# Four two-bank PSUM tiles, and the turn of P inside the next unit's scores, in the Transformer stages of a four-layer kernel

## The chip, the core and the metric

The kernel runs on one core of a Trainium2 chip. The time is the device time of one launch in microseconds (us); a comparison uses the median of several runs. Five engines work side by side, each through its own instructions in order: TensorE (PE in the profile, its weight loads PEld), VectorE (DVE), ScalarE (ACT), GpSimd (POOL) and SyncE (SP, here the queue that issues most transfers). Matrix products are written to PSUM, which has eight banks of 128 partitions by 512 float32 values; DVE and ACT read them from there.

## The reference

Four layers of the form `x = x + s * silu(f)` run over 2048 tokens of 128 features (four rows of 512 tokens). In each, `s` comes from an attention-like function of the normalised `x` and `f` from a feed-forward-like one. In two of the layers the latter is a small local-attention Transformer of its own, and these are all that the change touches:

```python
for i in range(DEPTH):                       # third layer: 6, 16 heads, window 32; fourth: 2, 8 heads, window 64
    h = shift_tokens(x)
    q, k, v = split(h @ Wqkv[i], 3)          # heads of 64
    q, k = l2norm(q) * qs, l2norm(k) * ks    # then rotated by position
    # each window of queries sees its own window of keys and the one before
    sim  = einsum('bhwie,bhwje->bhwij', q, look(k)) * 8.0
    attn = softmax(where(mask, -max, sim))
    out  = einsum('bhwij,bhwje->bhwie', attn, look(v))
    x = x + out @ Wo[i]
    h = layernorm(shift_tokens(x)) * g + b
    a, gate = split(h @ W1[i] + b1, 2)
    x = x + (a * gelu(gate)) @ W2[i] + b2
```

Everything is float32.

## The kernel before

The layers run one after another. The Transformers are built by the class `_Transformer`, called from `transformer` (L707). Features lie on partitions, so a row of the batch is a 128x512 tile.

Work is cut into slots. A slot is one layer, one row of the batch and one group of eight heads: 6 x 4 x 2 = 48 slots in the first Transformer, 2 x 4 x 1 = 8 in the second. Three Python generators walk through the slots, each some slots behind the one before it: `queries_keys` projects q and k, sums their squares over each head by a matmul with a matrix of ones (`unit_length`), rotates them, and sends them through 16 transfers to the tiles `qk`; `attention` computes the attention of the slot before; `feed_forward` does the feed-forward of a row some slots back. In the first Transformer one slot of a pair carries the norm of the feed-forward and the other its two matmuls W1 and W2.

`merge` (L947) sets the order in which the instructions are issued. Each generator yields after some work the TensorE time that it has just put down (0.86 for a 128x512 matmul, for instance), and the one that is least advanced goes next. A scheduler then places the instructions: it keeps near this order, but lets an instruction pass another whose data or tile it does not expect to be ready, and gives each tile of a pool the buffer that it expects to be free. The semaphores follow from that. The order on each engine is fixed when the program runs.

Inside `attention` a slot has two units, `j` = 0 and 1 (four units in the second Transformer). A unit goes through these steps:

- `scores` (L1361): a mask by two bfloat16 matmuls (L1366), then 64 small matmuls (64x32 weights, 64 columns) on top of it (L1377), all into one two-bank tile; then DVE takes the maximum of each row (L1387) and subtracts it (L1391), ACT takes the exponential (L1396), DVE sums (L1398) and inverts. The result is `P`.
- `turn` (L1403): eight transposes of P (recorded at L126, names `core,l_P`) into another two-bank tile, and ACT's copy of it to `PT` (L1412).
- `weigh` (L1414): 64 small matmuls of PT with the values into a tile, which DVE normalises into `On` (L1441).
- `turn_back` (L1452): transposes of On (`core,l_On`) and ACT's copy to `OT` (L1461); after the second unit four matmuls with Wo, and DVE adds them to the row of `xn` (L1501).

At step i of its loop `attention` issues `values` (first unit only; its tile is copied to `l_vo` by ACT at L1344) and the scores of unit i, then the turn of unit i-1, the turning back of unit i-2, and the weighing of unit i-1.

Nearly all matmuls pass through the helper `mm` and are recorded at L122, so they are told apart by names: `hb,l_wqk` is a projection of q or k, `sqp,l_k` the sums of squares, `l_wv,hb` the values, `l_OT,l_wo` the output projection, `ffu,l_w` the feed-forward's W2. On DVE, L1289 and L1291 multiply a projection by the two rotation tables (`l_rot`, `rotp`) and so read its tile out; L1316 scales `l_rot` by the length. L1287 on ACT squares the projection.

In PSUM a pool `ps` holds three tiles of two banks (`S2`) and a pool `pm` two tiles of one bank (`M`): eight banks. `M` serves the output projection and W2, and in the second Transformer also the weighing and the turning back.

## Time and profile before

| | us |
|---|---|
| median of 3 runs | 4267.34 (4264.73 to 4271.99) |
| the profiled execution, its own time | 4258.36 |
| its span, first to last instruction | 4256.7 |
| TensorE busy | 3632.9 (85%) |
| VectorE busy | 2521.8 (59%) |
| ScalarE busy | 1832.3 (43%) |
| GpSimd busy | 1200.4 (28%) |
| first Transformer, about | from 1605 to 3680 |
| second Transformer, about | from 3770 to 4230 |

A line of the profile gives the source line, engine, operation, `out<-in` by the program's names, and the shape. PE's rows count a float32 matmul as two passes, so that 64 matmuls are 128 rows; a transpose is one row. Behind a row of the timeline stands in brackets the idle time of its engine before it and the instruction that ended it; "issue" is idle time with nothing in the profile that was waited for. In a list of waits the columns are the total in us, how many times, and the longest.

### The profile page before, as it was taken

How to read it: one execution, taken by the hardware profiler on the slowest of the kernel's cores; microseconds unless marked ns; L12 is line 12 of the kernel's file. 1: busy time of each engine (PE TensorE's matmuls, PEld its weight loads, DVE VectorE, ACT ScalarE, POOL GpSimd, SP SyncE). 2: the span in 40 equal slices, each digit the busy share in tenths (PEclk: the TensorE clock that was granted, in tenths of full speed). 3: DMA queues.
4: the chain of work that ended last, by engine and by line, in shares of the span. 5: the costliest groups of instructions: out<-in, count | busy, mean ns of one | idle time of the engine just before them, and what ended most of it. 6: DMA issues, size and time to landing. Idle time of an engine off the chain costs nothing.

```text
span 4256.7 us, 105246 instructions
## 1 busy us (share of the span) xinstructions
PE 3632.9 (85%) x46765; PEld 1894.8 (45%) x46891; DVE 2521.8 (59%) x3429; ACT 1832.3 (43%) x2495; POOL 1200.4 (28%) x994
## 2 busy tenths in 40 slices
PE   7887999898999986888888888888888888768888
PEld 4554555344444433444444444444444444334444
DVE  6665555205433516677677777777667676447775
ACT  3344666331333343444444444444444444424554
POOL 1011444100111224333333433343333333033221
PEclk7678999996989988999999999999999999879999
DMA  1000000000000004334233424333333332222221
GB/s 35 7 24 26 1 1 1 28 10 7 1 3 2 1 15 113 85 81 106 70 89 98 95 67 120 70 86 94 86 73 92 87 85 69 75 85 68 58 63 43
DMA packets 123574, 236.11 MB, mean 55 GB/s; under 512 B 29625, under 2 KB 44129, under 8 KB 117729
## 3 DMA queue, kind: packets, MB, share of 16 engines
q1 hardware_dynamic: 114064, 209.58, 20.3%
q10 hardware_dynamic: 8624, 19.29, 1.4%
q8 instruction: 369, 6.05, 0.6%
q0 software_dynamic: 432, 0.51, 0.1%
q14 instruction: 85, 0.69, 0.1%
HBM read 50.08 MB, written 5.54 MB: 13 GB/s over the span
## 4 chain that ended last, share of the span: by engine, by line
PE 53%; DVE 16%; ACT 16%; issue 8%; POOL 3%; DMA 3%; SPq 1%; DVEq 0%; POOLq 0%; ACTq 0%
PE S L122 29%; PE M L122 8%; PE S L126 4%; PE S L1377 3%; PE o L1092 3%; DVE l_rot L1316 3%; DVE rotp L1291 3%; ACT l_P L581 3%; DVE l_rot L1289 2%; ACT l_PT L1412 2%; PE o L614 2%; ACT rn L1312 2%; POOL l_rot L1292 2%; ACT sqp L1287 1%; ACT l_P L1396 1%
## 5 line engine op out<-in xcount | busy, mean ns | idle before, releaser
L1292 POOL TENSOR_TENSOR l_rot<-l_rot,rotp 128x1024 f32<-128x1024 f32 x224 | 533.3, 2381 | 459.1 <-DVE rotp L1291 421.6
L1288 POOL TENSOR_TENSOR sqp<-sqp 128x512 f32<-128x512 f32 x224 | 315.6, 1410 | 1010.2 <-ACT sqp L1287 1009.6
L122 PE MATMUL S<-hb,l_wqk 128*128 128x512 f32 x896 | 501.4, 659 | 108.4 <-ACT l_vo L1344 32.3
L1287 ACT ACTIVATE sqp<-S 128x1024 f32<-128x1024 f32 x224 | 229.3, 1024 | 411.0 <-PE S L122 408.6
L1316 DVE SCALAR_TENSOR_TENSOR l_rot<-rn,l_rot 128x1024 f32<-128x1024 f32 x224 | 366.2, 1672 | 64.8 <-ACT rn L1313 62.3
L1289 DVE TENSOR_TENSOR l_rot<-S,l_tab 128x1024 f32<-128x1024 f32 x224 | 272.9, 1218 | 163.7 <-ACT sqp L1287 161.8
L126 PE MATMUL S<-core,l_P 128*128 128x128 f32 x1856 | 269.5, 288 | 57.3 <-DVE rotp L1291 13.5
L122 PE MATMUL S<-l_KT,l_QT 32*128 32x256 f32 (+7 forms) x1536 | 261.9, 505 | 34.8 <-ACT l_P L1114 14.2
L126 PEld LDWEIGHTS S<-core,l_P 128*128 128x128 f32 x1856 | 211.3, 146 | 177.2 <-issue 67.4
L1291 DVE TENSOR_TENSOR rotp<-S,l_tab 128x1024 f32<-128x1024 f32 x224 | 271.6, 1213 | 22.0 <-POOL l_rot L1292 21.8
L122 PE MATMUL S<-sqp,l_k 128*128 128x512 f32 x448 | 241.7, 633 | 33.3 <-POOL sqp L1288 24.9
L1114 ACT ACTIVATE l_P<-S 128x1024 f32<-128x1024 f32 x160 | 156.7, 1022 | 254.6 <-PE S L122 254.5
L1377 PE MATMUL S<-l_qk 64*32 64x64 f32 (+1 forms) x13312 | 222.1, 236 | 43.3 <-issue 34.3
L122 PEld LDWEIGHTS S<-hb,l_wqk 128*128 128x128 f32 x896 | 150.1, 199 | 244.0 <-issue 102.2
L122 PE MATMUL S<-l_wv,hb 128*64 128x256 f32 (+1 forms) x1600 | 237.1, 403 | 7.8 <-ACT rn L1312 2.4
L1377 PEld LDWEIGHTS S<-l_qk 64*32 64x32 f32 (+1 forms) x13312 | 174.1, 110 | 154.5 <-issue 151.0
L1412 ACT COPY l_PT<-S 128x1024 f32<-128x1024 f32 x128 | 129.5, 1012 | 250.1 <-PE S L126 250.0
L1067 DVE TENSOR_REDUCE l_mx<-S 128x2 f32<-128x768 f32 (+1 forms) x192 | 154.9, 863 | 134.1 <-PE S L1006 134.1
L1398 DVE TENSOR_REDUCE rs<-l_P 128x16 f32<-128x1024 f32 (+1 forms) x128 | 155.8, 1217 | 124.2 <-ACT l_P L1396 124.1
L122 PE MATMUL M<-l_OT,l_wo 128*128 128x512 f32 (+1 forms) x512 | 222.7, 546 | 4.1 <-ACT l_OT L1461 2.2
L1118 POOL TENSOR_SCALAR_AFFINE_SELECT l_P<-l_P 128x256 f32<-128x256 f32 x256 | 99.4, 406 | 409.9 <-ACT l_P L1114 405.1
L1387 DVE TENSOR_REDUCE mx<-S 128x16 f32<-128x1024 f32 (+1 forms) x128 | 155.7, 1217 | 98.7 <-PE S L1377 98.5
(359 smaller groups left out, 6619.9 us busy)
## 6 DMA issues: line engine op xcount, KB each, us to landing
l_qk<-l_rot SPq DMA_DIRECT2D x896, 128.0 KB
l_ve<-l_vo SPq DMA_DIRECT2D x112, 256.0 KB
l_ve<-l_vo SPq DMA_DIRECT2D x96, 224.0 KB
l_tab<-in_k_rot_l ACTq DMA_DIRECT2D x16, 1024.0 KB
l_wqk<-in_l2Wqkv SPq DMA_DIRECT2D x12, 512.0 KB
l_wv<-in_l2Wqkv SPq DMA_DIRECT2D x12, 256.0 KB
l_wo<-in_l2Wo SPq DMA_DIRECT2D x12, 256.0 KB
l_ve<-l_vo SPq DMA_DIRECT2D x24, 128.0 KB
```

The source lines that it names most:

```text
L122: self.nc.tensor.matmul(out, lhsT, rhs, start=start, stop=stop)
L126: self.nc.tensor.transpose(out, in_, self.ident[:n, :n])
L1114: nc.scalar.activation(P[u], s[u], AF.Exp, scale=scale)
L1287: nc.scalar.activation(sq, p, AF.Square)
L1288: nc.gpsimd.tensor_tensor(sq[:, 0, :], sq[:, 0, :], sq[:, 1, :], ALU.add)
L1289: nc.vector.tensor_tensor(t[:, g], p, tab[:, 0], ALU.mult)
L1291: nc.vector.tensor_tensor(m, p, tab[:, 1], ALU.mult)
L1292: nc.gpsimd.tensor_tensor(t[:, g], t[:, g], m[:, ::-1, :], ALU.add)
L1316: nc.vector.scalar_tensor_tensor(t[:, g], rn[:, g, :].unsqueeze(1).to_broadcast([128, 2, S]), 1e12, t[:, g], ALU.min, ALU.mult)
L1377: net.nc.tensor.matmul(sv[W * bl : W * bl + W, e, t, g, :].rearrange("p (s k) -> p s k", s=2), qk[0][r, g, j, W * c : W * c + W], kw, star ...
L1398: nc.vector.tensor_reduce(rs, P.rearrange("p t g e k -> p (t g e) k"), axis=AX.X, op=ALU.add)
L1412: self.nc.scalar.copy(u["PT"], t)
```

## The change

The pool of single banks goes, and the two-bank pool has four tiles instead of three. `M` takes a two-bank tile and uses its first bank. `turn` is now called inside `scores`: after half of the small matmuls of unit i (32 of 64 in the first Transformer), the eight transposes of unit i-1 and ACT's copy are issued, and then the other half. Only after the last unit, when there are no more scores, is it called on its own. `turn` itself now yields the 0.9 that `attention` yielded for it.

```diff
-            pools = [pool("ps", 3, space=PSUM), pool("pm", 2, space=PSUM), pool("c"), pool("tab", 3), pool("w")]
+            pools = [pool("ps", 4, space=PSUM), pool("c"), pool("tab", 3), pool("w")]
...
     def M(self):
-        return self.PM.tile([128, 512], F32, name="M", tag="M")
+        return self.S2()[:, 0, :]
...
-    def scores(self, qk, tp, j):
+    def scores(self, qk, tp, j, last):
...
         for t in range(T):
+            if last and t == T // 2:
+                yield from self.turn(last)
             for g in range(2):
...
         self.nc.scalar.copy(u["PT"], t)
+        yield 0.9
...
-                u["P"], u["r"] = yield from self.scores(qk, tp, j)
-            if last:
-                self.turn(last)
-                yield 0.9
+                u["P"], u["r"] = yield from self.scores(qk, tp, j, last)
+            elif last:
+                yield from self.turn(last)
```

The instructions of the changed program are the same in kind and number; which stands before which, and what each waits for, is not.

## The prediction

> **What bounds the kernel now.** I read the page first (busy shares, slices), then the stretches of the two Transformers, then TensorE's waits in the steady part of the first, then one slot's timeline. Last I laid the instruction order of the changed program beside the old one, engine by engine, with the instruction that each wait hangs on; the order holds no times, so all durations are from the trace.

> ```profile
> span 4256.7 us, 105246 instructions
> PE 3632.9 (85%) x46765; PEld 1894.8 (45%) x46891; DVE 2521.8 (59%) x3429; ACT 1832.3 (43%) x2495; POOL 1200.4 (28%) x994
> ...
> PE   7887999898999986888888888888888888768888
> ```

> TensorE is the busiest engine in all 40 slices but a few, never full. By stretch:

> ```profile
> core 0: us, PE busy (x) PEld busy (x) DVE busy (x) ACT busy (x) POOL busy (x), PEclk, DMA share, GB/s
> 1700.00:3640.00 1940.00, 1671.06 (x28271) 855.64 (x28362) 1367.93 (x1469) 886.41 (x1003) 697.26 (x407) 0.98 0.36 86
> 3770.00:4230.00 460.00, 380.66 (x3008) 215.88 (x3038) 320.75 (x384) 225.32 (x279) 128.42 (x82) 0.93 0.28 70
> ```

> The first row is the steady part of the six-layer Transformer (46 slots of 42.2 us, one slot being one row of the batch for half of the heads), the second the two-layer one. The clock is already 0.98, so nothing is to be had from it. The change removes no arithmetic: it can only move TensorE's idle time, 269 us in the first stretch and 79 in the second. Where those 269 come from:

> ```profile
> PE S L122 <- issue: 59.6, 36, 4.5
> PE S L126 <- ACT l_PT L1412: 45.1, 44, 1.1
> PE S L122 <- ACT l_vo L1344: 35.2, 45, 1.1
> PE S L1377 <- issue: 30.5, 38, 4.1
> PE S L122 <- DVE rotp L1291: 27.7, 37, 1.6
> PE S L126 <- DVE rotp L1291: 17.9, 29, 4.9
> PE S L122 <- POOL sqp L1288: 12.1, 23, 1.2
> PE S L126 <- DVE l_P L1391: 11.1, 22, 0.5
> ```

> (total us, times, longest.) Once a slot or once in two, the same wait: PSUM tiles not yet read out. Here is one slot; a float32 matmul is two rows, a transpose one:

> ```profile
> 2398.75 1.98 PE L122 MATMUL S<-hb,l_wqk 128*128 128x512 f32 x4 [0.90 <-ACT l_vo L1344]
> 2400.66 0.30 PE L1377 MATMUL S<-l_qk 64*32 64x64 f32 x2
> 2400.89 1.09 PE L126 MATMUL S<-core,l_P 128*128 128x128 f32 x8
> 2403.09 0.98 PE L126 MATMUL S<-core,l_On 128*128 128x128 f32 x7 [1.10 <-ACT l_PT L1412]
> 2404.00 1.47 PE L1377 MATMUL S<-l_qk 64*32 64x64 f32 x126
> 2405.51 1.22 DVE L1387 TENSOR_REDUCE mx<-S 128x16 f32<-128x1024 f32 x1 [1.26 <-PE S L1377]
> 2406.76 1.29 DVE L1391 TENSOR_TENSOR l_P<-S,mx 128x512 f32<-128x512 f32 x2
> 2408.09 1.06 ACT L1396 ACTIVATE l_P<-l_P 128x1024 f32<-128x1024 f32 x1 [1.25 <-DVE l_P L1391]
> 2410.79 1.02 PE L1377 MATMUL S<-l_qk 64*32 64x64 f32 x78
> ```

> See two things. The turn of O stands 1.10 us behind the copy of P's turn, for want of a third two-bank tile; and from the end of a unit's scores (2405.47) to its P being ready (2409.15) there are 3.7 us of DVE and ACT.

> **The change, part by part.** Slots alternate: in "hidden" slots the feed-forward's W1 and W2 run, in "norm" slots its norm. 23 of each.

> Pool. Five tiles (three of two banks, two of one) become four of two. It adds no bank. While scores, two projections and P's turn are held, O's turn is still the fifth. So by the order:
> - Projection after the mask (35.2 us, 45 times): it now waits for the copy of the first value tile, not the second; the second is waited for later, behind a 0.86 us matmul. Gain 33.
> - O's turn (45.1 us, 44 times): in hidden slots a projection (0.86) now stands between P's turn and O's; of 1.03 about 0.2 stays: gain 18. In norm slots the two are still adjacent and wait the same: 0.
> - Projection after the sums (the rotp row; about 23 of its 37, 1.0 each): it now hangs on the addition into xn, earlier on DVE; the values behind it hang on the normalised O, 0.4 later. Gain 0.6 x 23 = 14.
> - P's turn behind rotp (17.9 us): DVE no longer does the norm's operations before that rotp in norm slots. I take 10.
> - O's turn behind the second unit's subtraction (11.1, 22 times): it now waits for P's copy, issued half a unit earlier. Gain 11.
> Sum of gains 86.

> What comes late instead:
> - In hidden slots the third W1 pair reaches TensorE earlier and meets the first GELU product, which DVE makes after two l_rot of 1.67 each: 0.5 x 23 = 11. ACT then copies the values after the last GELU and a table load of 1.28 instead of before; the l_ve transfers on SP's queue issue later with it, some 4 us, and their readers stand over 10 us further on. POOL's additions keep their order; SP's 16 l_qk transfers a slot still follow l_rot, which is no later than before. I cost the queues at nothing; if that cover went, a late l_qk would hold the scores at about 1 us a slot.
> - W2's sum and Wo's hold a two-bank tile each, so the next slot's sums and projection wait for DVE's additions; by my count DVE is done 0.9 us before. Nothing. The output projection and the weighing hang on rotp in a few places: 0.35 per two slots, 8.

> Turning P amid the scores. TensorE runs in order, so behind the transposes the other 32 scores, a sum, O's turn and the projections are queued. After the first unit's scores the old order has a mean 6.7 us of work before its P is turned (64 weighings, two projections, mask, 64 scores, a sum, part of Wo). The new order has, in hidden slots, 31 weighings (0.75), mask (0.54), a projection (1.06) and 32 scores (0.75): 3.1 against 3.7 + 0.1, a wait of 0.6: 14 us over 23. In norm slots 48 weighings and a second projection bring it to 4.6: none. In the first three slots there are 32 scores alone: 3.0 each, 9 us. The second unit's P has 20 us of cover.

> Insertions. Full-array instructions are now put amid the small ones: P's eight, and a sum beside them. By the count over both orders there are 60 more such places in the first Transformer and 19 in the second. The row for one: 16 rows of scores at 2409.46, a projection at 2409.73, scores again at 2410.79, 1.33 us for 0.16 of scores and 0.86 to 0.97 of projection (the spacings of neighbouring 128x512 pairs, 2412.68 to 2413.65 to 2414.51), so 0.2 to 0.3. [...] I take the row.

> "issue" waits. 90 us fall inside runs of small matmuls, where no semaphore is waited for, and they recur every 256 instructions. [...] I take 15 less, near the smaller of the two rows, whose place the turn now takes.

> Second Transformer, 8 slots of 55 us: cover of the third unit falls from 4.2 to 2.4 us, where it waits 1.4 already: 1.8 x 8 = 14 more; the weighing's wait for P's copy shrinks by 0.9 and a projection's (1.1) goes: 16 less; insertions 5. Net +3.

> Sum: first Transformer -86 + 11 + 8 + 14 + 9 + 15 = -29; issue -15; second +3: -41. The profiled execution took 4258.4 (span 4256.7 and 1.7 around it): 4217. The median run is 9.0 above it: 4226.

> **Rivals.**
> 1. Slower: the softmax decides. If the first unit's maximum starts late on DVE (behind rotp or a normalisation), P's turn waits in every slot with everything queued behind it. For: 3.6 us of cover are given away. Against: the maximum starts 0.04 us after the scores in nearly every old slot, and what DVE is given ahead of it is ready earlier. It decides from 0.9 us a slot above my count (41/46). At 2 us: +92 - 41 = +51, 4318.
> [...]
> 3. A larger gain: issue waits and P's wait overlap (issue -50, P's 14 gone), and the small waits that I left standing go too (-15): -41 - 35 - 14 - 15 = -105, 4162.

> **How the numbers follow.** 0.2% (8 us) is about what a measurement of this kernel can tell from no change. Forecast 0.45, taking 4190 to 4258; larger gain 0.20; no change 0.08; slower 0.27. Faster 0.65, same 0.08, slower 0.27. The forecast's own range is 4190 to 4258; for 8 in 10 it must reach near rivals 1 and 3: 4150 to 4315.

> **What would show it.** After: no l_vo row at 35 us under TensorE's waits; the l_PT row at about half of 45 us; a new row of P's turn waiting for ACT's exponential, near 14 to 23 us; issue rows below 90. TensorE's busy time should stay within 25 us of 3633. The prediction is wrong if that exponential's row passes 60 us, if issue grows, or if DVE's rotp holds the projections that now share the one pool.

## The result, and the profile after

The changed kernel takes 4204.42 us in the median (4197.12 to 4208.22, 4 runs) against 4266.03 for the kernel before (4 runs as well, one more than in the table above); the ratio is 0.9854, interval 0.9834 to 0.9874. The forecast was 4226, within 4150 to 4315: the sign and the range hold, with a gain of 62 us where 41 were forecast. What follows shows that the agreement hides an incomplete account: one half of the change gains about 100 us, and the other half, as it stands here, loses about 45 of them again.

The page of the changed kernel:

```profile
span 4203.6 us, 105187 instructions
PE 3651.2 (87%) x46764; PEld 1923.0 (46%) x46891; DVE 2504.6 (60%) x3429; ACT 1842.0 (44%) x2495; POOL 1175.8 (28%) x994
```

TensorE is busy for 18 us more, in a span 53 us shorter. To compare like with like, take each Transformer from its first to its last matmul of scores, the same work in both kernels. First the kernel before, then the changed one (first Transformer, second Transformer; columns as in the prediction):

```profile
1639.60:3647.10 2007.50, 1716.64 (x29394) 881.51 (x29487) 1409.35 (x1510) 906.40 (x1023) 721.05 (x420) 0.98 0.36 86
3815.60:4204.00 388.40, 332.91 (x2832) 193.72 (x2860) 281.86 (x340) 200.56 (x247) 104.18 (x68) 0.95 0.27 63
```

```profile
1640.40:3586.70 1946.30, 1736.13 (x29372) 906.49 (x29470) 1397.06 (x1511) 914.34 (x1023) 690.64 (x419) 0.96 0.37 89
3754.10:4155.30 401.20, 341.27 (x2836) 198.89 (x2866) 278.13 (x341) 202.50 (x247) 107.73 (x68) 0.94 0.26 62
```

The first Transformer is 61 us shorter, the second 13 longer. Note the column behind the busy times: the granted clock is 0.96 where it was 0.98. TensorE's waits in the first stretch, some of the kernel before (over this stretch, a little longer than that of the prediction), then those of the changed one:

```profile
PE S L122 <- issue: 60.6, 37, 4.5
PE S L122 <- ACT l_vo L1344: 36.0, 46, 1.1
PE S L1377 <- issue: 33.8, 40, 4.1
PE S L122 <- DVE rotp L1291: 32.9, 38, 5.1
PE S L122 <- ACT l_OT L1461: 3.4, 9, 0.5
```

```profile
PE S L1380 <- issue: 42.0, 41, 3.1
PE S L126 <- ACT l_PT L1415: 30.1, 46, 1.1
PE S L122 <- DVE rotp L1291: 25.0, 22, 2.7
PE S L126 <- DVE rotp L1291: 22.8, 20, 1.5
PE S L122 <- issue: 22.8, 16, 2.2
PE S L122 <- POOL sqp L1288: 21.8, 44, 1.3
PE S L122 <- ACT l_OT L1465: 14.5, 25, 1.2
PE S L126 <- ACT l_P L1399: 13.3, 12, 2.8
PE S L1380 <- DMA l_qk<-l_rot: 8.7, 3, 7.4
```

The l_vo row is gone. The exponential holds P's turn for 13.3 us, and "issue" fell from 94.4 in the old kernel (60.6 and 33.8) to 64.8.

To separate causes I split each stretch into three parts that add up to its length. The trace's clock records know two values, full and half, in slices of 3.41 us or multiples of it; the clock column is their mean over a window. "Half-speed loss" is half of the time in which TensorE was busy within half-speed slices; "work at full clock" is its busy time less that loss; "idle" is the rest. An insertion is a change from the small matmuls (scores, weighing) to full-array work, counted in the trace. These parts are of the one profiled execution, which in e5_weigh took 22 us more than the median of its runs, and in e7_turn_weigh and e10_first_pairs 11 less; they agree with the views to 0.6 us. How far one execution can be trusted shows in e3_first, whose first Transformer is that of the changed kernel: its half-speed loss is 7 us more and its idle time 7 less.

| first Transformer, us | length | work at full clock | half-speed loss | idle | insertions | median |
|---|---|---|---|---|---|---|
| before | 2007.5 | 1680.9 | 35.9 | 290.7 | 351 | 4266.03 |
| changed | 1946.3 | 1678.8 | 58.0 | 209.6 | 411 | 4204.42 |
| e1_pool | 1907.2 | 1661.8 | 34.8 | 210.6 | 321 | 4158.31 |
| e2_turn | 2057.5 | 1691.9 | 60.9 | 304.8 | 439 | 4332.38 |
| e3_first | 1944.6 | 1676.8 | 65.1 | 202.7 | 411 | 4191.75 |
| e4_q3 | 1943.2 | 1665.3 | 58.7 | 219.3 | 364 | 4203.73 |
| e5_weigh | 1940.6 | 1651.9 | 66.6 | 222.1 | 253 | 4176.89 |
| e6_pairs | 1910.3 | 1627.0 | 80.2 | 203.1 | 239 | 4162.49 |
| e7_turn_weigh | 2003.2 | 1654.6 | 99.1 | 249.5 | 328 | 4269.03 |
| e8_pairs | 1854.3 | 1633.3 | 31.6 | 189.4 | 288 | 4105.15 |
| e9_warm | 2011.5 | 1774.5 | 44.5 | 192.6 | 417 | 4269.09 |
| e10_first_pairs | 1851.0 | 1634.4 | 28.4 | 188.2 | 288 | 4106.68 |
| e11_turn_pairs | 1851.6 | 1648.6 | 29.8 | 173.2 | 361 | 4105.57 |

### The profile page after: what moved, and what is told of

The parts are those of the page before. It is cut to its first block, busy times and chain, and to the rows that moved or that the text cites. A ratio compares the mean times of both kernels' runs of the same rounds, so it can differ in the third digit from the quotient of the medians.

```text
span 4203.6 us, 105187 instructions
## 1 busy us (share of the span) xinstructions
PE 3651.2 (87%) x46764; PEld 1923.0 (46%) x46891; DVE 2504.6 (60%) x3429; ACT 1842.0 (44%) x2495; POOL 1175.8 (28%) x994
## 4 chain that ended last, share of the span: by engine, by line
PE 64%; DVE 11%; ACT 10%; issue 6%; POOL 4%; DMA 3%; SPq 2%; POOLq 0%; DVEq 0%; ACTq 0%
PE S L122 41%; PE S L126 6%; PE S L1380 4%; PE M L122 4%; PE o L1092 3%; ACT l_P L581 3%; DVE l_rot L1316 2%; PE o L614 2%; POOL l_rot L1292 2%; POOL sqp L1288 2%; ACT sqp L1287 2%; SPq L1323 1%; DVE rotp L1291 1%; PE S L1006 1%; DMA l_qk<-l_rot 1%
## 5 line engine op out<-in xcount | busy, mean ns | idle before, releaser
L1288 POOL TENSOR_TENSOR sqp<-sqp 128x512 f32<-128x512 f32 x224 | 292.1, 1305 | 1001.8 <-ACT sqp L1287 995.6
L122 PE MATMUL S<-hb,l_wqk 128*128 128x512 f32 x896 | 497.8, 645 | 54.6 <-DMA l_wqk<-in_l3Wqkv 13.0
L1316 DVE SCALAR_TENSOR_TENSOR l_rot<-rn,l_rot 128x1024 f32<-128x1024 f32 x224 | 321.0, 1453 | 60.1 <-ACT rn L1313 57.7
L126 PE MATMUL S<-core,l_P 128*128 128x128 f32 x1856 | 274.6, 291 | 80.8 <-ACT l_P L1399 36.1
L1291 DVE TENSOR_TENSOR rotp<-S,l_tab 128x1024 f32<-128x1024 f32 x224 | 271.3, 1211 | 121.1 <-POOL l_rot L1292 121.1
L1380 PE MATMUL S<-l_qk 64*32 64x64 f32 (+1 forms) x13312 | 260.6, 246 | 71.4 <-issue 42.3
L126 PEld LDWEIGHTS S<-core,l_P 128*128 128x128 f32 x1856 | 215.5, 148 | 185.6 <-ACT l_P L1399 42.8
L122 PE MATMUL S<-l_KT,l_QT 32*128 32x256 f32 (+7 forms) x1536 | 265.7, 510 | 34.8 <-ACT l_P L1114 14.2
L1380 PEld LDWEIGHTS S<-l_qk 64*32 64x32 f32 (+1 forms) x13312 | 193.0, 115 | 210.0 <-issue 186.4
L122 PE MATMUL S<-sqp,l_k 128*128 128x512 f32 x448 | 246.9, 636 | 29.7 <-POOL sqp L1288 29.1
L1399 ACT ACTIVATE l_P<-l_P 128x1024 f32<-128x1024 f32 x128 | 134.8, 1053 | 292.8 <-DVE l_P L1394 292.5
L122 PEld LDWEIGHTS S<-l_ve,l_PT 64*32 64x32 f32 (+1 forms) x6656 | 170.8, 111 | 179.0 <-issue 119.4
L122 PE MATMUL S<-l_wv,hb 128*64 128x256 f32 (+1 forms) x1600 | 248.8, 402 | 1.9 <-ACT rn L1312 1.7
L122 PE MATMUL S<-l_ve,l_PT 64*32 64x64 f32 (+1 forms) x6656 | 215.9, 231 | 38.4 <-DVE rotp L1291 24.8
L122 PEld LDWEIGHTS S<-hb,l_wqk 128*128 128x128 f32 x896 | 156.4, 198 | 182.6 <-issue 120.5
L122 PE MATMUL S<-l_OT,l_wo 128*128 128x512 f32 (+1 forms) x512 | 223.8, 544 | 8.5 <-DVE ffu L1537 8.4
```

The lines of the kernel that those rows point to most:

```text
L122: self.nc.tensor.matmul(out, lhsT, rhs, start=start, stop=stop)
L126: self.nc.tensor.transpose(out, in_, self.ident[:n, :n])
L1288: nc.gpsimd.tensor_tensor(sq[:, 0, :], sq[:, 0, :], sq[:, 1, :], ALU.add)
L1291: nc.vector.tensor_tensor(m, p, tab[:, 1], ALU.mult)
L1316: nc.vector.scalar_tensor_tensor(t[:, g], rn[:, g, :].unsqueeze(1).to_broadcast([128, 2, S]), 1e12, t[:, g], ALU.min, ALU.mult)
L1380: net.nc.tensor.matmul(sv[W * bl : W * bl + W, e, t, g, :].rearrange("p (s k) -> p s k", s=2), qk[0][r, g, j, W * c : W * c + W], kw, star ...
```

## Experiments: one half at a time

**e1_pool**: four tiles, the turn at its old place.

```diff
-            if last and t == T // 2:
-                yield from self.turn(last)
...
-            elif last:
+            if last:
                 yield from self.turn(last)
```

> The pool alone: four two-bank tiles, P turned at its old place after the scores. Theory A (two separate gains that add up): the waits for a tile go as in the changed kernel (the l_vo row, 36 us, and part of the l_PT row, 45), the issue rows stay near the old 94 us because the turn no longer stands inside the scores; the first Transformer's scores stretch takes about 1970 us (old 2007, changed 1946), the median about 4230. Theory B (the tiles alone also take the issue waits away, because TensorE reaches its small matmuls at other times): issue below 75 us and a median near 4210. Theory C (the tiles bring nothing without the new place of the turn, the waits only move to the copy of P): above 4255.

Measured: 4158.31, ratio 0.9754 (0.9727 to 0.9781), 46 us under the changed kernel and beyond all three expectations. Its first stretch and the waits in it:

```profile
1647.70:3554.90 1907.20, 1696.37 (x29371) 893.86 (x29468) 1345.73 (x1509) 906.59 (x1022) 689.72 (x419) 0.98 0.38 91
```

```profile
PE S L122 <- issue: 55.8, 29, 3.4
PE S L1378 <- issue: 40.6, 40, 2.9
PE S L126 <- DVE rotp L1291: 32.9, 40, 1.2
PE S L122 <- POOL sqp L1288: 16.3, 39, 0.5
PE S L122 <- DVE rotp L1291: 15.0, 21, 1.4
PE S L122 <- ACT l_OT L1463: 14.6, 25, 1.2
PE S L126 <- ACT l_PT L1413: 7.2, 12, 1.1
```

The tiles alone bring the whole gain in idle time: 291 to 211 us, the same as in the changed kernel. The l_vo row (36.0) is gone and the l_PT row fell from 45.1 to 7.2. "issue" stays (96.4), as theory A said. Work at full clock is 19 us less, with 30 insertions fewer; what makes up most of the 19 is open.

**e2_turn**: the turn amid the scores, with the old tiles (the three lines of the pools put back).

> The turn amid the scores alone, with the old three and two tiles. Theory A (separate gains): the l_vo and l_PT rows stay (36 and 45 us), the issue rows fall by some 30 us to 65, insertions add about 20 us of TensorE's busy time and waits for the exponential about 13, the rotp rows in front of the turn fall: the median about 4255, 10 us under the old. Theory B (the issue waits are the pool's doing): issue stays near 94 and the median is 4270 to 4290, since only the costs are left. Theory C (three tiles are one too few for a turn amid the scores, each one holds a copy in front of the next scores): slower than 4300.

Measured: 4332.38, ratio 1.0169 (1.0143 to 1.0195): slower than the kernel before, so theory A fell and C had the size. Its largest waits in the first stretch, and the one that C named, for the copy of P:

```profile
PE S L122 <- issue: 54.5, 33, 4.6
PE S L122 <- ACT l_vo L1344: 35.9, 46, 1.1
PE S L126 <- ACT l_PT L1415: 34.7, 44, 1.1
PE S L122 <- DVE ffu L1537: 34.0, 22, 1.6
PE S L122 <- ACT l_PT L1415: 21.4, 41, 0.5
```

Issue fell by 8, not 30, and two rows grew: the third W1 pair behind the GELU product of the first, 22 times 1.5 us, and the sums of squares behind the copy of P, 21.4 us where the kernel before has 1.5. So a wait like C's is there, but it is the smaller of the two and does not stand in front of the next scores. Idle time grew by 14, work at full clock by 11 (88 more insertions), half-speed loss by 25. So the two halves are not two gains: the tiles are worth about 104 us in the median, the turn costs 46 with four tiles and 66 to 70 with three.

**e3_first**: the change in the first Transformer only.

```diff
-            pools = [pool("ps", 4, space=PSUM), ...]
+            pools = [pool("ps", 4 if heads == 16 else 3, space=PSUM)]
+            pools += [pools[0] if heads == 16 else pool("pm", 2, space=PSUM), ...]
...
-            if last and t == T // 2:
+            if self.split and last and t == T // 2:
...
```

> The change in the first Transformer only; the second keeps three two-bank and two single-bank tiles and turns P after the scores. Theory A (the second loses by the change: its scores stretch takes 401 us against the old 388, with 22.8 us of waits for the exponential against 11.3): about 4192, 12 below the changed kernel, the second stretch back at 388. Rival (the loss there is a single late transfer of l_qk, 10.2 us in the profiled run, that comes and goes whatever the order): within 4 us of the changed kernel, or a transfer wait of like size in the second stretch again.

Measured: 4191.75, ratio 0.9834 (0.9805 to 0.9863); the second stretch is back at 388.6 us. Theory A's 12 us are there (12.7 by the medians, 8.5 by the ratios), though the two ratios' intervals overlap, so that the stretch of the profile carries more of this than the times do. With the tiles alone this stretch takes 383.3 us, so there too the turn is the half that costs. But not by the wait for the exponential, to which theory A points; here are the kernel before, the changed one and e1_pool over the second stretch:

```profile
PE S L126 <- ACT l_P L1396: 11.3, 7, 4.4
PE S L126 <- ACT l_P L1399: 22.8, 13, 7.3
PE S L126 <- ACT l_P L1397: 18.6, 8, 7.3
```

Most of the growth is there with the turn at its old place. Split as above, the changed kernel's second stretch exceeds that of e1_pool by 8.3 us of work at full clock, 8.1 of half-speed loss and 1.5 of idle time. The rival's late transfer does not explain it either: e1_pool has one too (8.1 us against 10.8).

**e4_q3**: the turn after three quarters of the scores (`t == T - 1`).

> The turn after three quarters of the scores in the first Transformer (48 of 64), unchanged in the second, where half and three quarters fall on the same place (its scores have two parts). The exponential then has 16 more scores (0.38 us) of cover. Theory A (the ledger: only the waits for the exponential change): the 13 us of them in the first Transformer fall to about 5, the rest stays, 4196. [...]

Measured: 4203.73, ratio 0.9867 (0.9844 to 0.9889), no difference from the changed kernel. Its rows in the first stretch:

```profile
PE S L1380 <- issue: 51.6, 53, 3.1
PE S L122 <- issue: 26.4, 21, 2.3
PE S L126 <- ACT l_P L1399: 5.0, 6, 1.6
```

Theory A is half right: the exponential's wait fell from 13.3 to 5.0, but the rest did not stay, and issue grew from 64.8 to 78.0. Idle time as a whole is 10 us more and work at full clock 13.5 less, with 47 insertions fewer. The changed kernel's lower issue (65 against 96 in e1_pool) is no gain in the same way: l_PT (30.1 against 7.2), the exponential (13.3 against 2.0) and l_qk (8.7) stand in its place, and the idle sum is the same. What the "issue" waits are, no trace shows and no run tests.

## Experiments: what the turn amid the scores costs

The changed kernel is 39 us longer than e1_pool in the first Transformer: 17.0 more work at full clock, 23.2 more half-speed loss, 1.0 less idle. The granted clock of the whole kernel, on record for every run, agrees: 0.918 to 0.924 in the four runs of the changed kernel (mean 0.921), 0.924 to 0.930 in those of e1_pool (mean 0.926). I first took all of it for the price of 90 insertions, 0.45 each, and tested that by having fewer of them.

**e5_weigh** (on e1_pool) and **e7_turn_weigh** (on the changed kernel): a unit's weighing yields once.

```diff
-            yield 0.3 if self.split else 0.15
+        yield 2.4 if self.split else 0.6
```

> Four tiles, the turn at its old place, and the weighing of a unit yields once (2.4) instead of eight times (0.3), so that full-array matmuls are put between its 64 small ones less often: by the order 253 insertions in the first Transformer against 321 with the four tiles alone. Theory A (an insertion costs what the spacings of neighbours show, about 0.25 us): 17 us less, near 4141. Theory B (an insertion costs what the runs so far give when TensorE's busy time is set against the count, 0.45 us): 31 us less, near 4128. Rival (the interleaving covers waits: without it the maximum, the copy of P and the projections stand in TensorE's way): idle time of the first Transformer grows from 208 us by more than 20 and the median is at 4158 or above.

> The changed kernel, turn amid the scores included, with the weighing in one piece: 328 insertions against 412. Theory A (what the turn amid the scores costs is its insertions, 0.25 each): 21 us under the changed kernel, near 4183. Theory B (0.45 each): 38 us under it, near 4166, and so near the four tiles alone with 321 insertions, 4158. Rival (the turn costs by its place and not by the insertions, for example by the wait for the exponential with everything queued behind it): above 4195.

**e6_pairs**: as e5_weigh, and the projections and sums of a tile yield once for both.

```diff
                             net.mm(..., hk if i else hb)
-                            yield 0.86
+                        yield 1.72
...
             net.mm(p[:, g, :], self.ones, sums[g][:, 0, :])
-            yield 0.86
+        yield 1.72
```

> As the kernel with the weighing in one piece, and the two projections of a tile and the two sums of a tile also yield once for both (1.72), so that a tile is filled without a stop: 239 insertions. Theory A: 14 insertions fewer than with the weighing alone at 0.25 are 3 us; and tiles are held shorter, so that waits for tiles fall somewhat: 4125 to 4140. Theory B at 0.45: 6 us, 4115 to 4125. Rival (with pairs the squares and rotations of both halves come later, and DVE and POOL, which work through 4 us for a tile, hold up the sums and the next tile): rotp and sqp rows over 80 us together, against 64 with the four tiles alone, and a median over 4150.

Measured: e5_weigh 4176.89 (ratio 0.9809, 0.9765 to 0.9852), e7_turn_weigh 4269.03 (1.0016, 1.0003 to 1.003) and e6_pairs 4162.49 (0.9743, 0.969 to 0.9796). The work at full clock did fall, by 10, 24 and 35 us. But e5_weigh is some 19 us slower than e1_pool by the medians (their intervals overlap a little), and e7_turn_weigh loses the whole gain of the change. The medians are where the rivals put them, by another cause: the half-speed loss is 67, 99 and 80 us where e1_pool has 35. In e5_weigh idle time grew by 11 us, not by more than 20, and a single late load of weights is 13 of it; in e6_pairs the rotp and sqp rows fell instead of rising (14.6 us together). Only in e7_turn_weigh is the rival's wait there too, 44.1 us for the exponential.

```profile
PE S L122 <- DMA l_wv<-in_l2Wqkv: 13.1, 1, 13.1
```

Where does the clock fall? One place in the changed kernel, cut at the clock's own slices, and TensorE's timeline over it:

```profile
2498.03:2501.44 3.41, 2.35 (x11) 1.04 (x9) 3.23 (x4) 2.34 (x3) 0.42 (x1) 1.00 0.85 199
2501.44:2504.85 3.41, 1.94 (x15) 1.20 (x13) 0.91 (x2) 1.35 (x2) 3.16 (x2) 1.00 1.03 247
2504.85:2508.27 3.42, 2.35 (x146) 2.11 (x146) 3.38 (x3) 0.74 (x2) 2.34 (x1) 0.50 0.33 82
2508.27:2511.68 3.41, 2.57 (x30) 0.89 (x38) 2.31 (x4) 0.00 (x0) 0.03 (x1) 0.50 0.02 5
2511.68:2515.09 3.41, 3.05 (x114) 2.06 (x107) 2.45 (x4) 1.06 (x1) 0.00 (x0) 0.50 0.03 5
```

```profile
2500.81 0.87 PE L126 MATMUL S<-core,l_P 128*128 128x128 f32 x6 [1.06 <-DVE rotp L1291]
2501.62 0.30 PE L1380 MATMUL S<-l_qk 64*32 64x64 f32 x2
2501.84 0.44 PE L126 MATMUL S<-core,l_P 128*128 128x128 f32 x2
2503.38 1.09 PE L126 MATMUL S<-core,l_On 128*128 128x128 f32 x8 [1.10 <-ACT l_PT L1415]
2505.91 0.32 PE L122 MATMUL S<-l_ve,l_PT 64*32 64x64 f32 x2 [1.43 <-DVE rotp L1291]
...
2509.50 2.07 PE L122 MATMUL S<-hb,l_wqk 128*128 128x512 f32 x2
```

In the slice from 2501.44 TensorE is busy for 1.94 of 3.41 us: the end of P's turn, two rows of scores and O's turn, with a wait for P's copy between the turns and the start of a wait for rotp behind them. The next three slices run at half speed (0.50), and the projection at 2509.50 takes 2.07 us, where the one at 2494.07, at a clock of 1.00, takes 1.13. TensorE's 7.97 us of work in these three slices lost about 4 us. What precedes a fall shows when every full-speed slice of the first Transformer is counted in the thirteen traces (the two kernels and the eleven experiments):

| TensorE busy in a full-speed slice of 3.41 us | slices | followed by half speed |
|---|---|---|
| under 1.5 us | 242 | 236 |
| 1.5 to 2.0 us, mostly transposes | 75 | 59 |
| 1.5 to 2.0 us, mostly other matmuls | 236 | 30 |
| 2.0 us or more | 6357 | 0 |

So in these traces the clock fell after slices in which TensorE waited for about half of the time or more, after 236 of 242 with under 1.5 us of busy time; between 1.5 and 2.0 us it fell more often where the work was transposes (59 of 75 against 30 of 236). (The profile models the ends of matmuls, so these limits are rough.) Transfers, at a share of 0.85 and 1.03 in the slices from 2498.03 and 2501.44, are not the mark: their median share before a fall is 0.02 in e1_pool. A lack of large matmuls (projections, sums, values, Wo, feed-forward) is not enough: 197 of the 6357 slices of the last line hold none. The two expectations that follow rest on that narrower reading, which came from the medians: large matmuls held 0.0 us of the slice before a fall in the changed kernel and 2.2 to 2.6 us of full-speed slices that were followed by another.

The longest wait in the slice before a fall is "issue" in 19 of the 20 falls of e1_pool. In the changed kernel it is the wait for P's copy in front of O's turn in 13 of 26, "issue" in 8 and rotp in 4; 17 of the 26 slices hold mostly transposes, against 2 of 20. That is the place shown above: the turn of P now stands close to that of O, each with a wait at its side, and both fall into one slice.

**e9_warm**: needless large matmuls just ahead of the turn of the first unit, in the changed kernel.

```diff
+        if self.split and u["j"] == 0:
+            for i in range(4):
+                net.mm(t[:, 2 * i : 2 * i + 2, :]..., self.ones, self.k)
         for i in range(8):
             net.transpose(t[:, i, :], Pc[:, i, :])
```

> The changed kernel with four needless float32 matmuls of 128x256 (constants only) in front of the turn of each first unit in the first Transformer, into the tile of the turn, 0.43 us each: 48 x 1.72 = 83 us of added work, in the stretch where the half-speed slices of the changed kernel mostly begin. Theory A (a slice runs at half speed because the one before it held hardly any large matmul): half-speed time of the first Transformer falls from 137 us to 80 or less, which gives back some 25 us, and the waits for the exponential (13) are covered by the added work: about 4204 + 83 - 25 - 13 = 4249. Rival (the clock falls because of the load itself, for instance more activity in less time): half-speed time stays at 137 or grows, and the median is 4272 or more.

Measured: 4269.09, ratio 1.0014 (1.0003 to 1.0024); half-speed time 102 us against 137, its loss 44.5 against 58.0, while the work at full clock grew by 96. The exponential's wait went to 1.8. More load and less half-speed time: the load itself is not the cause. But the decrease is smaller than expected, the added matmuls cost 13 us more than their own 83, and the median is 20 us above theory A. The falls that are left begin elsewhere: of the 20 slices before them none holds a turn with added matmuls in front, and twelve hold a turn without them, as in the place shown above. Nor does this run tell a large matmul from any work that fills a waiting slice, since the slices with under 2.0 us of busy time fell too, from 45 to 35.

**e8_pairs**: four tiles, old place of the turn, projections and sums in pairs, the weighing in eight pieces again.

> Four tiles, the turn at its old place, the weighing again in eight pieces, and only the projections and the sums of a tile in pairs: 288 insertions against 321 with the four tiles alone and 239 with the weighing in one piece as well. Theory A (an insertion costs about 0.27 us at the full clock, and the half-speed slices come where TensorE has no large matmul for some 3.4 us, which a weighing in pieces avoids): TensorE's work at full clock is 9 us under the four tiles' 1659, the half-speed time back near their 74 us from the 170 of the kernel with both edits; first Transformer about 1893, median 4140 to 4150. Rival (pairs by themselves leave long stretches without a large matmul): half-speed time over 130 us and a median of 4160 or more.

Measured: 4105.15, ratio 0.9626 (0.9603 to 0.9649), better than theory A.

```profile
1641.00:3495.30 1854.30, 1664.66 (x29377) 900.88 (x29471) 1380.81 (x1509) 895.10 (x1022) 712.22 (x419) 0.98 0.39 93
```

```profile
PE S L1378 <- issue: 64.8, 51, 3.4
PE S L122 <- issue: 56.0, 35, 3.4
PE S L122 <- DVE rotp L1291: 6.3, 11, 0.6
PE S L126 <- DVE rotp L1291: 4.9, 18, 1.1
```

The clock is back (half-speed time 69 us against 170 in e6_pairs), and the two differ in the weighing alone, so its one piece was what cost it. Pairs lower the work at full clock by 28 us, more than 33 insertions explain; why is open. The rotp rows and the sqp row come to 12 us together, where e1_pool has 64. That a tile filled without a stop is free again sooner would fit, but is a guess; when each tile came free was not compared. What is left is mostly issue, 121 us.

**e10_first_pairs** (pairs in the first Transformer only) and **e11_turn_pairs** (pairs, and the turn amid the scores):

```diff
+                            if not self.split:
+                                yield 0.86
+                        if self.split:
+                            yield 1.72
```

> Four tiles, the turn at its old place, projections and sums in pairs in the first Transformer only. The second then has the order of the four tiles alone, whose scores stretch took 383.3 us against 390.9 with pairs. Theory A (the two Transformers are independent of each other): 7.6 us under the kernel with pairs in both, near 4098. Rival (the difference of the second is chance, such as where the half-speed slices fall): within 3 us of it.

> The changed kernel, turn amid the scores included, with projections and sums in pairs: 361 insertions in the first Transformer against 288 with pairs and the turn at its old place. Theory A (the turn amid the scores costs the same whatever the rest of the order: in the first Transformer some 12 to 17 us of TensorE's work at full clock, some 23 by more half-speed time, nothing in idle time, and about 10 in the second): near 4152, and half-speed time of the first Transformer near 130 us against 69. Rival (the loss came from the order around it, and pairs make up for it): 4120 or less.

Measured: e10_first_pairs 4106.68 (ratio 0.9643, 0.9609 to 0.9677) and e11_turn_pairs 4105.57 (0.9637, 0.9605 to 0.967). e10_first_pairs is not told apart from e8_pairs: its second stretch is 378.9 us in the profile against 390.9, but the medians don't show it. TensorE's issue waits and the wait for P's copy in e11_turn_pairs:

```profile
PE S L122 <- issue: 44.4, 34, 3.3
PE S L1380 <- issue: 35.9, 33, 2.6
PE S L126 <- ACT l_PT L1415: 3.5, 3, 1.2
```

e11_turn_pairs overturns theory A: with pairs the turn amid the scores costs nothing. The table splits that: 15.3 us more work at full clock for 73 insertions (0.21 each; 17.0 for 90 in the changed kernel, 0.19 each), half-speed loss the same, and idle 16 less (issue is 38 less, 82 against 121, where the 82 include 2.1 in front of transposes, and other waits took back 22). The price of the insertions is real and small; the half-speed loss was a matter of the order around the turn. The wait for P's copy, the main one in the slices before the changed kernel's falls, is 3.5 us here against 30.1, and the falls are 12 against 26. No order tried makes the turn amid the scores a gain.

## Why the prediction was right, and where it was not

The median was 22 us lower than forecast, inside the range. By its own steps, in the first Transformer:

- **The pool's gains** were put at 86 with the turn's. The projection after the mask: 33 forecast, 36 measured. O's turn behind P's copy: 18 forecast; 15 in the changed kernel, 38 in e1_pool. The projection after the sums: 14 forecast, 8 (25.0 left of 32.9). O's turn behind the subtraction: 11 and 11. P's turn behind rotp: 10 forecast, nearly none (22.8 left of 23.4). (What O's turn waited for was a free two-bank tile, not a third one: the pool had three.)
- **The costs**: the third W1 pair was put at 11; it waits in e2_turn (34.0) but not in the changed kernel (0.2). P's wait for the exponential: 23 forecast, 13. (In its hidden-slot sum 3.7 + 0.1 less 3.1 is 0.7, not 0.6, so 16 us and not 14.) The values' copy and the queues behind it were put at nothing, and the late l_qk rows cost 9. Waits for tiles held longer were put at nothing too; the row for the copy to OT grew from 3.4 to 14.5 (14.6 with the tiles alone) and the sqp row from 14.2 to 21.8.
- **Insertions**: 60 forecast and 60 counted, at 0.25 (15 us), the middle of what the row at 2409.46 gave (0.2 to 0.3). Against e1_pool the turn's cost is 0.19 each, and 0.21 with pairs. Against the kernel before, work at full clock still comes out 2 us less, because the pool alone took 19 off, only in part by its 30 insertions fewer.
- **The issue waits** were put at 15 less, an estimate of mine that no run shows; they are 30 less (94.4 to 64.8). But e1_pool and e4_q3 show other waits growing where they shrink and the reverse, so the term should not have been added to the others as a gain. Their spacing is in the traces: in the first Transformer, the 56 of the kernel before that are longer than 0.4 us stand 254 to 2557 of TensorE's recorded instructions (matmuls, weight loads, semaphores) apart, every distance a multiple of 254 to 256, and so are all those between the 43 of the changed kernel. Why, the traces do not show.
- **The failed step** is the sentence that with a clock of 0.98 nothing is to be had from it. 22 us were to be lost (35.9 to 58.0), the largest single cost of the change, and it stood in none of the cases. What the runs show in its place: P's turn and O's, each with a wait, fall into one slice of 3.41 us, and at the place shown the clock was 0.50 in the three slices behind it. This is also why rival 1, which had the turn as the losing half, named the wrong mechanism: the exponential takes 13 us, the clock 22.
- **The second Transformer** was put at +3 and cost 13: 6 of work, 2 of half-speed loss, 4 idle. Its waits for the exponential grew by 11.5, near the 14 of that step, but by luck: 7.3 of them come with the tiles alone. The gains set against it did not show as less idle time.

The signs that it named came out as follows: the l_vo row is gone, l_PT is at two thirds and not half of 45, the exponential's row is at 13.3 where 14 to 23 were named, and issue is below 90; rotp still holds the projections, for 25 us, 8 less than before. So the size agreed in part by luck: a term left out (22) and a second Transformer mis-sized (10) stood against an issue term, a wait and insertions that came out lighter.

## What to carry to other kernels

When a change has two halves, price each alone: here four equal tiles were worth about 100 us, and moving the turn among the small matmuls spent almost half of that. Before changing the order in which small and large matmuls are mixed, look at the clock column slice by slice: where TensorE was busy for less than 1.5 us of a 3.41 us slice, the next one nearly always ran at half speed here (236 of 242), and up to 2.0 us it sometimes did (89 of 311), so two short waits that fall together can cost more than their sum: at the place shown, two waits of 1.10 and 1.43 us went with about 4 us of loss. And try having the two matmuls that fill one tile issued together: here that alone was worth about 53 us on top of the four tiles.
